# One shared group, one more SyncE group and later column starts in a message-passing layer whose rows come by four ways

## The chip, the cores and the metric

The kernel runs on one core of a Trainium2 chip. The metric is the device time of one execution in microseconds (us); three executions of the kernel before took 3390.92, 3395.1 and 3396.24 us, median 3395.1 us. The profile shows one more execution, which took 3398.46 us and whose span from the first to the last instruction is 3396.4 us. In the profile PE is TensorE, DVE is VectorE, ACT is ScalarE, POOL is GpSimd and SP is SyncE.

## The reference

A graph has N = 12,500 nodes with 128 features and E = 400,000 edges, sorted by their target `dst`, each with 32 features. One layer is computed:

```
h   = relu(layernorm(x))
m   = relu([h[src], h[dst], edge_attr] @ w1 + b1) @ w2 + b2      # one row for each edge
agg = segment_sum(m, dst)
gi, gh = agg @ w_ih + b_ih,  h @ w_hh + b_hh
r, z, n = sigmoid(i_r + h_r), sigmoid(i_z + h_z), tanh(i_n + r * h_n)
out = x + (1 - z) * n + z * h
```

## The kernel before

**Stages.** A first stage normalises the nodes, leaves h transposed on the chip (`hT_all`, 128 features by 12,500 nodes) and stores A = h @ w1[:128] and B = h @ w1[128:256] + b1 in device memory. Because `dst` is sorted, B's rows for an edge are taken from a short window of nodes. What remains per edge is a row of A at `src`, which is random access. The edges are cut in tiles of 128; eight tiles make a group k (`PAIR`), 391 groups in all (`NP`), the first with five tiles. The main loop has two units per group, `NU` = 782 units u, and a group k is worked on in units 2k and 2k+1, with its stages some units ahead.

**Four ways for the source rows.** The dictionary `mode` says for a group k who brings its rows:

- no entry: GpSimd gathers them with eight indirect DMAs (`gather`, L163), one per tile, into one of 11 buffers `G` (`GBUFS`). These groups are listed in `ring`; group i of the ring waits until group i - 11 has been used. The first nine groups (`RAW`) are gathered from x instead of A and normalised in the loop.
- `"act"`: ScalarE copies 1,024 columns of `hT_all`, one each instruction (L979, `one_by_one`), into a tile `HE_act`. The numbers of the columns come from the tile `at` by register loads, 16 at a time (L961).
- `"dve"`: VectorE does the same two columns at a time (L986, which packs two columns' bytes), loads 32 registers at a time, and after each 128 columns unpacks them into `HE_dve` (L991).
- `"sp"`: SyncE issues 1,024 DMAs of one 512-byte row of A each (L968), into the single buffer `G_sp`.

**What follows.** `pre` (L683, L694) forms the edge's pre-activation in PSUM: the window of B and the edge features by one matmul, and for `act` and `dve` groups also w1a against the columns brought. `add` (L713) is a VectorE operation that adds G and takes the relu for gathered and SyncE groups; for `act` and `dve` groups the relu is one ScalarE activation instead (L725, `relu`). `seg` (L739) sums by target with one-hot matrices made by VectorE (L586, L633); every 14 groups a block of nodes goes through the gates in small steps (`node`).

**Order.** Nothing is reordered: every engine takes its instructions as the program writes them. Which groups go to whom is fixed by `SPREAD` (how many groups each engine brings), `START` (the unit in which its first job begins) and the loop at L91, which spreads the groups of an engine evenly from `START`/2 + 2 to a last place. A job for group k runs from the end of the engine's job before it to unit 2k - 4 (SyncE: 2k - 8, and its next job begins at 2k + 2, since it has one buffer). `run_jobs` deals a job's steps out evenly over its units, in four phases a unit, between the other stages. The window rows (L613) and the tiles `L` (L574, L577) are also SyncE's, in the same queue as its rows.

Before, ScalarE brings 29 groups (16, 29, 42, 56, ... 374, 388), VectorE 28 (20, 34, 47, ... 372, 386), SyncE 4 (105, 197, 287, 379); 330 groups remain for GpSimd.

Of the kernel before, what the change touches and what calls it, by code (L numbers as in the profile page):

```python
# [9 lines left out]
F32 = mybir.dt.float32  # L10
# [14 lines left out]
PAIR = 2 * GRP  # L25
# [26 lines left out]
LOAD = {"act": 16, "dve": 32, "sp": 32}  # L52
PIECE = 128
STEP = {"act": 4, "dve": 8, "sp": 4}
ROW = 4 * D
SPREAD = {"dve": 28, "act": 29, "sp": 4}
START = {"dve": 10, "act": 2, "sp": 24}
NR = 12672

H_AT = 16512  # L60

# [2 lines left out]
def tile_gnn(ctx: ExitStack, tc: tile.TileContext, x, src, srcT, dstT, dstP, eaT, eaP, w1, b1, w2T, b2,  # L64
# [10 lines left out]
    pj = late.enter_context(tc.tile_pool(name="pj", bufs=2, side="right"))  # L75
# [12 lines left out]
        return [(t0 + a * GRP + j, j, a) for j in (2 * h, 2 * h + 1) for a in range(2)  # L88
                if t0 + a * GRP + j < t1]

    mode, order = {}, {m: [] for m in SPREAD}  # L91
    for m, n in SPREAD.items():
        lo, hi = START[m] // 2 + 2, NP - {"dve": 5, "act": 3, "sp": 12}[m]
        for i in range(n):
            k = lo + int((i + 1) * (hi - lo) / n)
            while k in mode:
                k += 1
            mode[k] = m
            order[m].append(k)


# [33 lines left out]
    stats = dram.tile([N, 2], F32, name="stats")  # L135
    S = dram.tile([NR, D + 1], F32, name="S")
    B = dram.tile([N, D], F32, name="B")
# [51 lines left out]
    nc.vector.memset(brow, 0.0)  # L189
    b1b = const.tile([128, D], F32, name="b1b")  # L190
    base_d = at[96:97, :NP - 1]
    by_hand = [k for m in ("sp", "act", "dve") for k in order[m]]
    NJ = len(by_hand)
    place_of = const.tile([NJ, 2], F32, name="place_of")
    for i, (to_sp, to_others) in enumerate(((ROW, 4), (0, H_AT))):
# [346 lines left out]
    def check_windows():  # L542
        m = const.tile([128, 2], F32, name="lim1")
        nc.vector.tensor_reduce(m[:, 0:1], lim[:, 0, :], AX.X, ALU.max)
        nc.vector.tensor_reduce(m[:, 1:2], lim[:, 1, :], AX.X, ALU.min)
        bad = const.tile([128, 2], F32, name="bad")
        nc.vector.tensor_scalar(bad[:, 0:1], m[:, 0:1], float(V - 1), None, op0=ALU.is_gt)
        nc.vector.tensor_scalar(bad[:, 1:2], m[:, 1:2], 0.0, None, op0=ALU.is_lt)
        one = const.tile([128, 1], F32, name="one")
        nc.vector.tensor_tensor(one, bad[:, 0:1], bad[:, 1:2], op=ALU.max)  # L550
        pm = SEGB[1][:, 384:512]
        nc.tensor.transpose(pm[0:1, :128], one, ident)
        f = const.tile([1, 8], F32, name="flags")
        nc.vector.tensor_reduce(f[:, 0:1], pm[0:1, :128], AX.X, ALU.max)
        nc.vector.tensor_reduce(f[:, 1:2], off_f, AX.XY, ALU.max)
        nc.vector.tensor_reduce(f[:, 2:3], step_f, AX.X, ALU.max)
        nc.vector.tensor_scalar(f[:, 3:4], blk_f[:, NB - 1:NB], float(N - BLOCKS[-1][2]), None,
                                op0=ALU.not_equal)
        nc.vector.tensor_copy(f[:, 4:5], beyond)
        nc.vector.tensor_reduce(f[:, 6:7], f[:, 0:5], AX.X, ALU.max)  # L560
        nc.vector.tensor_copy(flag, f[:, 6:7])
# [3 lines left out]
    hand = {}  # L565
# [380 lines left out]
    def column(v):  # L946
        return h_bytes[:, bass.ds(v - H_AT, 4)]

    def one_by_one(m, k):
        et = {"act": ET.Activation, "dve": ET.DVE, "sp": ET.SP}[m]  # L950
        r = by_hand.index(k)
        if m == "sp":
            goal[k] = tc.alloc_semaphore(f"brought{r}"), 16 * PAIR * 128
            G[k] = pj.tile([128, GRP, 2, D], F32, name="G_sp", bufs=1)
            rows = G[k].bitcast(U8)
        else:
            hand[k] = pj.tile([128, PAIR * 128], F32, name=f"HE_{m}")
            he = hand[k].bitcast(U8)
        for e0 in range(0, PAIR * 128, LOAD[m]):
            low, high = (0, ROW * (N - 1)) if m == "sp" else (H_AT, H_AT + 4 * (N - 1))  # L960
            _, vals = nc.values_load_multi_w_load_instructions(  # L961
                at[r:r + 1, e0:e0 + LOAD[m]], engines=[et], min_val=low, max_val=high,
                skip_runtime_bounds_check_because="src holds numbers of nodes")
            if m == "sp":
                for i, v in enumerate(vals):
                    e = e0 + i
                    a, j = divmod(e // 128, GRP)
                    fetched = nc.sync.dma_start(rows[e % 128:e % 128 + 1, j, a, :],  # L968
                                                A_bytes[bass.ds(v, ROW)].rearrange("(o f) -> o f", o=1))
                    fetched.then_inc(goal[k][0], 16)  # L970
                    tc.no_tile_sem_insts.add(fetched.ins.name)
                    tc.add_to_no_dep_group(f"rows{k}", fetched.ins)
                    if i % STEP[m] == STEP[m] - 1:
                        yield
                continue
            if m == "act":
                for i, v in enumerate(vals):
                    e = e0 + i
                    nc.scalar.copy(he[:, e * 4:e * 4 + 4], column(v))  # L979
                    if i % STEP[m] == STEP[m] - 1:  # L980
                        yield
                continue
            if e0 % PIECE == 0:
                both = pj.tile([128, PIECE // 2, 4], U16, name="both")
            for i in range(0, LOAD[m], 2):
                nc.vector.scalar_tensor_tensor(both[:, (e0 % PIECE + i) // 2, :], column(vals[i + 1]),  # L986
                                               256.0, column(vals[i]), op0=ALU.mult, op1=ALU.add)
                if i % STEP[m] == STEP[m] - 2:
                    if (e0 + i + 2) % PIECE == 0:
                        p0 = e0 + LOAD[m] - PIECE  # L990
                        nc.vector.tensor_copy(  # L991
                            he[:, p0 * 4:(p0 + PIECE) * 4].rearrange("p (n c b) -> p n c b", c=2, b=4),
                            both.bitcast(U8).rearrange("p n (b c) -> p n c b", c=2))
                    yield

    jobs = {}
    for m, kl in order.items():
        start = START[m]
        for k in kl:
# [3 lines left out]
    live = {}  # L1003
# [3 lines left out]
    def run_jobs(u, phase):  # L1007
        if phase == 0:
            for m, k, span in jobs.get(u, ()):
                live[m] = [one_by_one(m, k), u, span, PAIR * 128 // STEP[m], 0]  # L1010
        for m, job in list(live.items()):
            it, start, span, steps, done = job
            want = -(-steps * ((u - start) * PH + phase + 1) // (span * PH))
            while job[4] < want:
                job[4] += 1
                if next(it, "end") == "end":
                    del live[m]
                    break
# [56 lines left out]
    for u in range(NU):  # L1075
        k, h = divmod(u, 2)
        gathers(u)
        if h == 0:
# [14 lines left out]
            if k == NP - 20:  # L1093
                check_windows()
        if u == min(START.values()) - 2:
            nc.vector.tensor_scalar(at[:NJ, :], at[:NJ, :], place_of[:, 0:1], place_of[:, 1:2],
                                    op0=ALU.mult, op1=ALU.add)

        def other(phase):
            run_jobs(u, phase)  # L1100
            if h == 0 and phase == 3:
                take(k - 1)
            if phase == 3:
                step(nodes_left)
                if u in LAST_STEPS:
                    next(last)
# [114 lines left out]
    f = nc.values_load(flag[0:1, 0:1], min_val=0, max_val=1)  # L1221
# [67 lines left out]
```

## Time and profile before

| | us |
|---|---|
| median of three executions | 3395.1 |
| the profiled execution | 3398.46 |
| its span | 3396.4 |
| busy: PE / DVE / ACT / POOL | 2410.5 / 2254.8 / 3183.8 / 2536.6 |

A line of the profile's groups names the line of the code, the engine, the operation, its output and inputs, and how often it ran; then the time busy, the mean duration of one in ns, and the idle time of its engine just before it with what ended most of that. "Issue" is idle time that ended without anything that the profile shows; on VectorE and ScalarE the register loads of L961 lie in it, since they are not counted as busy. In a table of waits a row has the total, the number and the longest. A row of the timeline has the start, the duration, the instruction with its count, and the idle time before it in brackets. Busy time of copies that overlap in the pipeline is counted once, so the cost of one is the busy time divided by the count and not the mean duration.

### The profile page before, as it was taken

The page shows a single profiled execution, that of the slowest core. Times are in us where ns is not written, and L with a number is a line of the kernel's source. Part 1 is how long each engine was busy: PE and PEld are TensorE (multiplying, and loading weights), DVE is VectorE, ACT ScalarE, POOL GpSimd, SP SyncE. Part 2 cuts the span into 40 slices and gives each one's busy share as a digit, 9 for nine tenths or more (in the row PEclk, how much of TensorE's full clock was granted, in tenths as well). Part 3 has the DMA queues.
Part 4 walks back from the last instruction along what each step waited for, and adds up shares of the span by engine and source line. Part 5 has one row for each costly group of instructions (what it writes and reads, how often), then busy time and mean ns, then how long its engine had stood idle before and what let it go on. Part 6 is the DMA issues. An engine that isn't in the chain of part 4 may idle for free. (4 is left out here: it accounts for less than half of the span.)

```text
span 3396.4 us, 92978 instructions
## 1 busy us (share of the span) xinstructions
PE 2410.5 (71%) x13145; PEld 1547.7 (46%) x13145; DVE 2254.8 (66%) x16792; ACT 3183.8 (94%) x30083; POOL 2536.6 (75%) x2646
## 2 busy tenths in 40 slices
PE   7568767776677677677767776776676577767767
PEld 7445434444444344444444443454444344444445
DVE  8566667667666676676666666666666666666665
ACT  7699999999999999899999999999998999999995
POOL 7767777777777777777777777777777777777774
PEclk9777778877878788787778778777777887778878
DMA  6333444434434444343344343443443433444432
GB/s 214 97 85 87 101 99 95 99 94 106 95 96 98 99 97 96 95 103 95 92 100 97 92 100 94 102 93 97 97 102 87 101 94 94 100 100 96 94 94 62
DMA packets 194428, 334.67 MB, mean 99 GB/s; under 512 B 68293, under 2 KB 115972, under 8 KB 193809
## 3 DMA queue, kind: packets, MB, share of 16 engines
q0 software_dynamic: 84384, 172.99, 22.8%
q1 hardware_dynamic: 109281, 155.66, 17.2%
q14 instruction: 510, 4.18, 0.4%
q8 instruction: 109, 1.79, 0.2%
q10 hardware_dynamic: 144, 0.07, 0.0%
HBM read 308.21 MB, written 20.24 MB: 97 GB/s over the span
## 5 line engine op out<-in xcount | busy, mean ns | idle before, releaser
L163 POOL DMA_INDIRECT G<-A,src_i x2568 | 2469.5, 962 | 803.0 <-issue 761.5
L979 ACT COPY HE_act<-hT_all 128x4 uint8 x29696 | 2993.9, 189 | 52.9 <-issue 27.2
L986 DVE SCALAR_TENSOR_TENSOR both<-hT_all 128x4 uint16 x14336 | 1214.1, 154 | 990.4 <-issue 980.6
L683 PE MATMUL pre<-RW,L 128*128 128x256 f32 x3128 | 1130.2, 487 | 217.0 <-DVE RB L713 200.4
L683 PEld LDWEIGHTS pre<-RW,L 128*128 128x128 f32 x3128 | 662.5, 236 | 500.2 <-DVE RB L713 216.2
L739 PE MATMUL seg<-RB,OH 128*32 128x129 f32 x6250 | 609.4, 326 | 308.1 <-DVE RB L713 238.9
L739 PEld LDWEIGHTS seg<-RB,OH 128*32 128x32 f32 x6250 | 334.8, 126 | 802.2 <-DVE RB L713 460.3
L713 DVE CUSTOM_DVE_ANT_0 RB<-pre,G 128x1024 f32<-128x1024 f32 x322 | 389.4, 1210 | 26.0 <-PE pre L683 21.6
L734 PE MATMUL seg<-zrow 1*128 1x129 bf16 x196 | 45.9, 234 | 215.0 <-DVE OH L633 212.7
L586 DVE TENSOR_SCALAR L<-L,node_of 64x512 f32<-64x512 int32 x382 | 188.7, 494 | 10.7 <-DMA L<-in_dstP 10.7
L633 DVE TENSOR_TENSOR OH<-dloc,seg 128x512 f32<-128x512 f16 (+1 forms) x198 | 132.2, 668 | 0.0
L765 PE MATMUL nd<-spot,sums 128*128 128x40 f32 x782 | 114.5, 316 | 4.8 <-DVE sums L748 4.7
L765 PEld LDWEIGHTS nd<-spot,sums 128*128 128x128 f32 x782 | 109.8, 226 | 14.4 <-issue 8.8
L991 DVE COPY HE_dve<-both 128x512 uint8<-128x512 uint8 x224 | 102.4, 457 | 7.7
L848 PE MATMUL nd<-ident,gt 128*128 128x128 f32 (+2 forms) x112 | 28.5, 400 | 98.0 <-DVE gt L844 88.0
L694 PEld LDWEIGHTS pre<-w1a,HE_act 128*128 128x128 f32 x464 | 82.0, 221 | 9.5
L244 PE MATMUL nd<-w1b,hT_all 128*128 128x128 f32 x224 | 45.5, 346 | 56.5 <-DVE xb L850 56.5
L694 PEld LDWEIGHTS pre<-w1a,HE_dve 128*128 128x128 f32 x448 | 78.8, 220 | 9.2
L163 POOL DMA_INDIRECT G<-in_x,src_i x69 | 65.7, 952 | 21.9 <-issue 20.7
L694 PE MATMUL pre<-w1a,HE_act 128*128 128x128 f32 x464 | 80.5, 302 | 0.0
L725 ACT ACTIVATE RB<-pre 128x1024 f32<-128x1024 f32 x66 | 66.8, 1013 | 13.2 <-PE pre L694 13.2
L694 PE MATMUL pre<-w1a,HE_dve 128*128 128x128 f32 x448 | 77.7, 302 | 0.0
(177 smaller groups left out, 1374.9 us busy)
## 6 DMA issues: line engine op xcount, KB each, us to landing
G_sp<-A SPq DMA_DIRECT2D x4096, 0.5 KB
L<-in_dstP SPq DMA_DIRECT2D x195, 256.0 KB
L<-in_eaP SPq DMA_DIRECT2D x195, 256.0 KB
G<-A,src_i POOLq DMA_INDIRECT x2568, 2.6
RW<-B SPq DMA_DIRECT2D x782, 16.0 KB
xb<-in_x SPq DMA_DIRECT2D x26, 256.0 KB
out<-xb SPq DMA_DIRECT2D x26, 256.0 KB
xs<-in_x SPq DMA_DIRECT2D x11, 512.0 KB
```

Of the source, the lines that this page charges most:

```text
L163: fetched = nc.gpsimd.indirect_dma_start(out=G[k][:, j, a, :], out_offset=None, in_=table, in_offset=bass.IndirectOffsetOnAxis(ap=src_i[c] ...
L586: nc.vector.tensor_scalar(o, i, node_of[:, k:k + 1], None, op0=ALU.is_equal)
L633: nc.vector.tensor_tensor(p, dloc[:, e0:e1, None].to_broadcast(shape), row[:, None, :].to_broadcast(shape), op=ALU.is_equal)
L683: nc.tensor.matmul(p[:, 2 * i:2 * i + 2, :], Ls[k // QP][:, c0:c0 + 128], RW[k % 4], start=True, stop=not raw)
L694: nc.tensor.matmul(p[:, 2 * i + a, :], cols, w1a, start=False, stop=n + 1 == len(l) or l[n + 1][1] != j)
L713: made = nc.vector._custom_dve(TENSOR_ADD_SAT, out=o, in0=p, in1=G[k].rearrange("p j a f -> p (j a) f")[:, c, :], s0=float("inf"), s1=0.0)
L725: nc.scalar.activation(o, p, AF.Relu)
L739: nc.tensor.matmul(p[r0:r0 + V, :D + 1], OH[k][:, a * GRP + j, :], RB[k % 2][:, 2 * j + a, :D + 1], start=False, stop=all(b != a for _, _, ...
L765: nc.tensor.matmul(p[:, bass.ds(offs[i], V + SHIFT)], sums[:, slot(b, i), :D], spot[:, i % 2, :], start=False, stop=i == len(offs) - 1)
L979: nc.scalar.copy(he[:, e * 4:e * 4 + 4], column(v))
L986: nc.vector.scalar_tensor_tensor(both[:, (e0 % PIECE + i) // 2, :], column(vals[i + 1]), 256.0, column(vals[i]), op0=ALU.mult, op1=ALU.add)
L991: nc.vector.tensor_copy(he[:, p0 * 4:(p0 + PIECE) * 4].rearrange("p (n c b) -> p n c b", c=2, b=4), both.bitcast(U8).rearrange("p n (b c) ...
```

## The change

Group 197, before a SyncE group, becomes a shared one: ScalarE brings its first 512 columns and VectorE its last 512, into one tile `HE_dve`. ScalarE brings 28 whole groups beside it, VectorE 27, SyncE 5. The first job of VectorE begins in unit 14 instead of 10, that of ScalarE in unit 4 instead of 2. The places are now spread on either side of 197 separately. The number of groups that GpSimd gathers stays 330.

The places are now, for ScalarE: 17, 30, 43, 57, ... 177, 191, (197), 211, 225, ... 374, 388; for VectorE: 22, 36, 50, 64, ... 176, 190, (197), 210, 224, 237, ... 372, 386; for SyncE: 87, 160, 233, 307, 379. After 197 each group of VectorE stands one or two places before one of ScalarE.

```
-SPREAD = {"dve": 28, "act": 29, "sp": 4}
-START = {"dve": 10, "act": 2, "sp": 24}
+SPREAD = {"dve": 27, "act": 28, "sp": 5}
+START = {"dve": 14, "act": 4, "sp": 24}
+MIDDLE = 197
...
-    mode, order = {}, {m: [] for m in SPREAD}
+    mode, order = {MIDDLE: "both"}, {m: [] for m in SPREAD}
     for m, n in SPREAD.items():
         lo, hi = START[m] // 2 + 2, NP - {"dve": 5, "act": 3, "sp": 12}[m]
-        for i in range(n):
-            k = lo + int((i + 1) * (hi - lo) / n)
-            while k in mode:
+        n1, mid = (0, lo) if m == "sp" else (n // 2, MIDDLE)
+        places = [lo + int((i + 1) * (mid - lo) / (n1 + 0.5)) for i in range(n1)] + [MIDDLE] * (m != "sp")
+        for k in places + [mid + int((i + 1) * (hi - mid) / (n - n1)) for i in range(n - n1)]:
+            while k != MIDDLE and k in mode:
                 k += 1
-            mode[k] = m
+            mode.setdefault(k, m)
             order[m].append(k)
...
+    def share(m, k):
+        half = PAIR * 64
+        return (0, 2 * half) if k != MIDDLE else (0, half) if m == "act" else (half, 2 * half)
...
-            hand[k] = pj.tile([128, PAIR * 128], F32, name=f"HE_{m}")
+            if k not in hand:
+                hand[k] = pj.tile([128, PAIR * 128], F32, name="HE_dve" if k == MIDDLE else f"HE_{m}")
...
-        for e0 in range(0, PAIR * 128, LOAD[m]):
+        for e0 in range(*share(m, k), LOAD[m]):
...
-                live[m] = [one_by_one(m, k), u, span, PAIR * 128 // STEP[m], 0]
+                e0, e1 = share(m, k)
+                live[m] = [one_by_one(m, k), u, span, (e1 - e0) // STEP[m], 0]
```

More of the change, by code (lines that the diff above doesn't have):

```diff
@@ L191, in tile_gnn @@
     base_d = at[96:97, :NP - 1]
-    by_hand = [k for m in ("sp", "act", "dve") for k in order[m]]
+    by_hand = order["sp"] + order["act"] + [k for k in order["dve"] if k != MIDDLE]
     NJ = len(by_hand)
```

## The prediction

> **What bounds the kernel now.** I read the page's groups first, for what each engine does and how often.
>
> ```profile
> span 3396.4 us, 92978 instructions
> PE 2410.5 (71%) x13145; PEld 1547.7 (46%) x13145; DVE 2254.8 (66%) x16792; ACT 3183.8 (94%) x30083; POOL 2536.6 (75%) x2646
> L163 POOL DMA_INDIRECT G<-A,src_i x2568 | 2469.5, 962 | 803.0 <-issue 761.5
> L979 ACT COPY HE_act<-hT_all 128x4 uint8 x29696 | 2993.9, 189 | 52.9 <-issue 27.2
> L986 DVE SCALAR_TENSOR_TENSOR both<-hT_all 128x4 uint16 x14336 | 1214.1, 154 | 990.4 <-issue 980.6
> ```
>
> ACT looks like the limit at 94%. DVE has 980.6 us of "issue" besides its 2254.8 busy: that is its register loads, so it is near 95% too. POOL's 75% misleads: behind each gather stand some 0.3 us of issue. POOL's own timeline, with the line's own view, shows this:
>
> ```profile
> L163 POOL DMA_INDIRECT G<-A,src_i x2568: 942/947/1624, 92.9 to 3361.3; - x198
> DMA to landing us min/median/max: 2.5/2.7/5.5
> ...
> 215.62 0.95 POOL L163 DMA_INDIRECT G<-A,src_i  x1 [7.75 <-DVE RB L713]
> 216.87 0.95 POOL L163 DMA_INDIRECT G<-A,src_i  x1 [0.30 <-issue]
> ...
> 331.02 0.94 POOL L163 DMA_INDIRECT G<-A,src_i  x1 [4.36 <-DVE RB L713]
> ...
> 3361.32 0.95 POOL L163 DMA_INDIRECT G<-A,src_i  x1 [0.31 <-DMA G<-A,src_i]
> ```
>
> One gather starts every 1.25 us (216.87 - 215.62), and after 331.02 POOL never again stands still for a buffer: all its waits for anything but issue come before that. So POOL is a clock that runs through to 3361.32 whatever the others do. Who uses the rows?
>
> ```profile
> 3376.27 1.29 DVE L713 CUSTOM_DVE_ANT_0 RB<-pre,G 128x512 f32<-128x512 f32 x2 [3.12 <-PE pre L683]
> ...
> 3380.30 0.63 PE L739 MATMUL seg<-RB,OH 128*32 128x129 f32 x8
> ```
>
> The last group's rows land at about 3361.32 + 2.7 = 3364.0, and its add starts at 3376.27, released by PE and not by the landing. So the users of the rows are 12 us behind POOL at the end, and **they set the end**; POOL is just ahead. The windows and waits of the two long stretches, before and after group 197's place, say which user:
>
> ```profile
> 330.00:1710.00 1380.00, 993.19 (x5391) 622.77 (x5391) 928.54 (x7080) 1328.87 (x12929) 1047.52 (x1087) 0.79 0.41 97
> 1710.00:3330.00 1620.00, 1137.47 (x6226) 716.23 (x6226) 1076.97 (x8189) 1553.84 (x14986) 1229.31 (x1280) 0.79 0.40 97
> ...
> DVE both L986 <- issue: 424.1, 362, 2.4
> ACT gt L824 <- PE nd L818: 26.0, 7, 7.3
> PE seg L739 <- DVE RB L713: 119.9, 75, 5.0
> PE seg L739 <- ACT RB L725: 15.7, 6, 4.1
> ...
> DVE both L986 <- issue: 505.5, 415, 2.5
> PE seg L739 <- DVE RB L713: 113.0, 70, 7.6
> PE seg L739 <- ACT RB L725: 27.5, 10, 5.8
> ```
>
> The first four waits are of 330 to 1710, the last three of 1710 to 3330. DVE is taken for (928.54 + 424.1)/1380 = 98.0% of the first stretch and (1076.97 + 505.5)/1620 = 97.7% of the second, ACT for 96.3% and 95.9%. PE's `seg` waits for DVE some eight and four times as long as for ACT. So DVE limits, with ACT 2% behind it.
>
> **The change, part by part.** *Less work.* ScalarE's copy costs 2993.9/29696 = 0.101 us; 512 fewer are 51.6 us. Half a DVE group is 256 packing operations at 1214.1/14336 = 0.085 us, 16 register loads at 980.6/896 = 1.09 us (28 groups of 1,024 columns, 32 a load, are 896 loads) and four unpackings: 21.7 + 17.5 + 1.8 = 41 us.
>
> ```profile
> L991 DVE COPY HE_dve<-both 128x512 uint8<-128x512 uint8 x224 | 102.4, 457 | 7.7
> L713 DVE CUSTOM_DVE_ANT_0 RB<-pre,G 128x1024 f32<-128x1024 f32 x322 | 389.4, 1210 | 26.0 <-PE pre L683 21.6
> ```
>
> One group more is added by DVE (1.2 us), and ACT has one activation fewer. POOL keeps its 330 groups: nothing.
>
> *Where it goes.* The places decide. Before, DVE has a group every 13.5, ACT every 13.3. After, up to 197 DVE has one every 14 and ACT still one every 13.3; behind 197 DVE has one every 13.5 again and ACT one every 13.65. So **DVE is relieved in the first half alone and ACT in the second alone.** In the first stretch, 334 units (54 to 388), DVE gives up 1.1 of 37.8 columns a unit: 334 x 1.1 x 41/512 = 29 us. ACT is unchanged there and has 51 us idle (1380 - 1328.87), most of it such waits as the 26.0 at the gates, which a faster DVE shortens in part. The bounds are 0 and 51; I take 14, half of what DVE gives up, since ACT is 2% behind. In the second stretch, 376 units, ACT gives up 376 x 1.03 x 0.101 = 39 us and DVE takes up 4 (0.1 column a unit and the add). What ACT's relief can end is PE's 27.5 us of waits for it, and DVE stands between: from 4 us worse to 24 us better, taken as 9.
>
> *The later starts.* ACT is full early on:
>
> ```profile
> 137.00:215.00 78.00, 52.91 (x332) 42.39 (x330) 47.61 (x310) 77.73 (x609) 52.80 (x55) 0.81 0.32 81
> 215.00:330.00 115.00, 85.73 (x441) 52.76 (x439) 73.81 (x563) 114.03 (x1107) 83.88 (x88) 0.77 0.37 86
> ```
>
> Two units without copies take 2 x 39 x 0.101 = 7.9 us from it before the wait that ended at 215.62; without copies such a unit is left to the normalising chain, so I take half, 4, with 0 and 7.9 as bounds. DVE's four units gain nothing while ACT is full. POOL gains too: the wait that ended at 215.62 shrinks by 4, and the one at 331.02 goes, since one hand-brought group instead of two now stands before the buffer in question, and an earlier add frees it: 4.36 - 0.30 = 4.1. POOL ends 8 us earlier (bounds 4 and 12).
>
> *SyncE.* Its queue carries the window rows and L too, so what it adds counts:
>
> ```profile
> 1608.55 3.55 SPq L968 DMA_DIRECT2D G_sp<-A  x10
> ...
> L961 SPq TENSOR_LOAD <-at x128: 1872/2148/2357, 238.4 to 3247.9; - x128
> ...
> SPq L574 <- PE pre L683: 407.1, 94, 14.9
> SPq L613 <- PE pre L683: 165.4, 36, 19.1
> SPq L574 <- PE pre L694: 71.5, 16, 12.3
> ```
>
> A row costs 3.55/10 = 0.355 and a 32nd of a 2.15 us load: 0.42 us, a group 432 us. SyncE's waits for PE, time in which it is early, are 407.1 + 165.4 + 71.5 = 644 us. They hide it, with 212 us left over; where a stretch lacks cover, L and the window rows come late, and `onehot_T` on DVE and `pre` on PE wait for them. L is asked for six units ahead, 6 x 4.13 us (1380/334), so I take nothing; the price if the cover is gone is a rival below.
>
> *Group 197.* ACT brings 512 columns in 12 units, 42.7 a unit instead of some 37.5: 6 us late at most, once, and one unit of slack stands behind it. PE waits for two engines where it waited for one. Nothing to 6 us; I take nothing.
>
> *The sum.* The users of the rows: 4 + 14 + 9 = 27 us, which would end the span at 3369. But POOL now stands in front of them. Its last gather starts at 3361.32 - 8 = 3353.3, lands at 3356.0, is added by 3357.3 (1.29), and from the first `seg` of the last group to the end stand 3396.4 - 3380.30 = 16.1 us: **3373.4 is the floor.** The two routes are nearly equal, and users that run close to POOL's landings lose some to each wait; half of a group's time, 5 us, is my allowance. 3378.5 is 18 us under the span. The profiled execution took 3398.46, 3.4 over the median of 3395.1, so I take the 18 us from the median: about 3378.
>
> The Trainium skill, "DMA: Bandwidth & Descriptors", section "Issuing engines are not separate DMA queues", says that DMAs from SyncE and GpSimd run on the same 16 engines and interleave, which speaks against 1,024 more rows. By that rule the last landing could be up to 5.5 instead of 2.7 us behind its gather, and the floor 3 us later; the windows' DMA share of 0.41 and 0.40, with four SyncE groups already under way, gives it little weight.
>
> **The rivals.**
>
> *No difference.* The engine that is not relieved holds each half: ACT the first (it is at 96.3%), DVE the second (97.7%). For it: each has under 4% idle. Against: PE waits little for ACT in the first half. Then only the early 4 us and a few are won: 3391, between 3388 and 3400.
>
> *Slower: SyncE becomes the limit.* Its jobs of 1,024 rows last 170 to 178 units before and 134 to 142 after, so it issues up to 7.5 rows a unit instead of 6.
>
> ```profile
> 1607.33 1.12 SPq L613 DMA_DIRECT2D RW<-B  x2
> ```
>
> At 0.42 us a row 7.5 rows are 3.15 us; the window rows are 1.12 us for two units, and I take as much again for L and the nodes' DMAs less a tenth, 1 us a unit: 4.15 us of the first half's 4.13. That little is carried by the lead of some 20 us with which L and the window rows are asked for, and each job begins anew. It decides from about 0.44 us a row, where 136 units run late by more than the lead. At 0.46 the first two jobs lose 6 and 23 us (142 x 0.18 - 20, 136 x 0.32 - 20), and PE and DVE wait as long: 3395 + 29 = 3424, from 3402 up. The second half's units, 1620/376 = 4.31 us, still have room. Against: the 644 us of early time.
>
> *ACT alone is the limit.* Then all of its 51.6 us come back: 3343. Against: POOL's clock, which would have to end 30 us earlier than it can. The Trainium skill, "Perfetto Trace Analysis", section "Identifying the Most-Contended Engine", names the engine with the highest occupancy, here ACT at 94%, as the one to relieve; the trace disagrees by POOL's unbroken spacing of 1.25 us at 75%.
>
> *The change does not do what it says*: half a group late at 197 costs more than it saves. Once 6 us against 27: it ends as no difference.
>
> **How the numbers follow.** The forecast, POOL and the users near each other: 0.62, from 3368 (POOL's waits all but gone, 12 us, and no allowance) to 3387. No difference, with 197's delay: 0.22, of which 0.04 falls just under 3388 and 0.02 over 3402. SyncE: 0.11. ACT alone: 0.02. Left over: 0.03, to either side. 0.2% is 6.8 us, about what a measurement of this kernel can tell from no change. Faster is 0.62 + 0.04 + 0.02 + 0.02 = 0.70, the same 0.16, slower 0.11 + 0.02 + 0.01 = 0.14. The range reaches from 3368 to 3398, over most of the rival of no difference.
>
> **What the next profile would show.** If right: POOL's last gather starts near 3353, its wait near 215 is about 4 us shorter and the one near 331 gone; the last group's add follows its landing within a few us; DVE's taken share falls in the first half, ACT's in the second; SyncE's waits for PE fall from 644 to about 200 us; VectorE has begun to wait for landings. Wrong, if DVE or PE wait for L or RW by more than 20 us in all, if PE's waits at group 197's matmuls exceed 6 us, or if the lag at the last add stays at 12 us.

## The result, and the profile after

The changed kernel takes 3382.5 us (median of 6 runs, 3379.91 to 3388.39), beside 3395.67 us for the kernel before on the same chip (6 runs, 3390.92 to 3402.74). The ratio is 0.9961, with a 95% interval of 0.9946 to 0.9976: **13.2 us or 0.39% faster**. The forecast was 3378, in a range of 3368 to 3398. The profiled execution took 3383.67 us; it was 3398.46 before.

The page of the changed kernel, first its busy times, then its groups (lines were added to the file: L163 is now L165, L613 is L615, L713 is L715, L739 is L741, SyncE's row L968 is L975, ScalarE's copy L979 is L986 and VectorE's L986 is L993):

```profile
span 3381.8 us, 94224 instructions
PE 2384.9 (71%) x13129; PEld 1538.3 (45%) x13129; DVE 2230.9 (66%) x16533; ACT 3132.6 (93%) x29570; POOL 2532.8 (75%) x2646
L165 POOL DMA_INDIRECT G<-A,src_i x2568 | 2465.5, 960 | 787.1 <-issue 762.3
L986 ACT COPY HE_act<-hT_all 128x4 uint8 x28672 | 2889.2, 189 | 50.6 <-issue 26.8
L993 DVE SCALAR_TENSOR_TENSOR both<-hT_all 128x4 uint16 x14080 | 1192.8, 154 | 969.4 <-issue 961.2
```

The removed work is there at the foretold size: VectorE has 21.3 us fewer of packing and 19.4 fewer of register loads, ScalarE 51 fewer in all (512 of its copies now write `HE_dve` and aren't in the line above). POOL's idle time fell from 803.0 to 787.1 us, and its gathers together from 2469.5 to 2465.5. That makes POOL 19.9 us earlier. Most of it is its waits for buffers, before and after:

```profile
POOL G L163 <- DVE RB L713: 16.4, 14, 7.7
...
POOL G L165 <- DVE RB L715: 2.8, 7, 1.0
```

The two waits of 7.75 and 4.36 us that the prediction named are both gone. The timeline, POOL's last gather and VectorE's last add, shows where this leads:

```profile
3341.53 0.94 POOL L165 DMA_INDIRECT G<-A,src_i  x1 [0.30 <-issue]
...
3360.73 1.29 DVE L715 CUSTOM_DVE_ANT_0 RB<-pre,G 128x512 f32<-128x512 f32 x2 [3.10 <-PE pre L685]
```

The last gather starts 19.8 us earlier than before (3361.32), the last add only 15.5 (3376.27). With 2.7 us to landing, the median of the kernel before, the add comes 16.5 us behind its rows, where it was 12.3. So the users of the rows still set the end, and POOL is farther ahead of them than it was.

The windows of the two long stretches (span, then busy us of PE, PEld, DVE, ACT, POOL, granted clock, DMA share, GB/s), and the waits in them, first those of 330 to 1710, then those of 1710 to 3330:

```profile
330.00:1710.00 1380.00, 965.19 (x5449) 613.55 (x5446) 922.20 (x6947) 1340.11 (x13025) 1047.70 (x1090) 0.81 0.42 99
1710.00:3330.00 1620.00, 1148.61 (x6194) 721.82 (x6194) 1068.83 (x8143) 1503.72 (x14503) 1229.38 (x1282) 0.78 0.41 97
```

```profile
DVE both L993 <- issue: 399.0, 344, 2.9
DVE L L588 <- DMA L<-in_dstP: 42.1, 16, 6.4
...
PE pre L685 <- DMA RW<-B: 145.6, 42, 7.3
...
PE seg L741 <- DVE RB L715: 57.6, 37, 4.2
...
PE seg L741 <- ACT RB L727: 35.5, 12, 6.1
...
DVE both L993 <- issue: 517.0, 410, 2.6
...
ACT gt L826 <- PE nd L820: 67.6, 14, 11.8
```

In the first stretch VectorE's taken share fell from 98.0% to (922.20 + 399.0)/1380 = 95.7%, as foretold, but a new wait for the tiles L, 42.1 us, brings it to 98.8%. PE waits less for VectorE (57.6 us, before 119.9), and 145.6 us for window rows (RW in the lines). Both L and the window rows are SyncE's. In the second stretch VectorE is as full as before, (1068.83 + 517.0)/1620 = 97.9%, while ScalarE has gone from 95.9 to 92.8%: its relief turned up as waiting, 67.6 us of it at the gates (28.6 before). PE waits there for window rows too, 34.7 us, where before it had no such wait.

SyncE's own waits for PE in the first stretch say why L came late. Before:

```profile
SPq L574 <- PE pre L683: 151.9, 37, 14.9
SPq L613 <- PE pre L683: 36.9, 12, 9.1
...
SPq L574 <- PE pre L694: 22.2, 6, 7.6
```

After:

```profile
SPq L576 <- PE pre L685: 11.3, 8, 5.1
SPq L615 <- PE pre L685: 5.1, 1, 5.1
```

Of 211.0 us in which SyncE was early 16.4 are left, 194.6 fewer. The rows that it issued in this stretch, before and after:

```profile
L968 SPq DMA_DIRECT2D G_sp<-A x1894: 224/228/706, 330.0 to 1709.8; - x190
...
L975 SPq DMA_DIRECT2D G_sp<-A x2356: 212/228/561, 329.8 to 1709.3; - x197
```

The 462 rows more, at the prediction's 0.42 us a row, are 194 us, just what SyncE lost of its early time. The prediction set its new load against the 644 us of the whole kernel. Over the whole kernel its sum holds well (109.7 + 88.6 + 36.3 = 235 us are left of 644, some 200 were foretold), and in the first stretch it fails.

A table of where the users stand, from the starts of a group's add in each trace, after less before in us (negative is earlier). SP4, STARTS, DVE27 and ACT28 are experiments below:

```
group      9     60    100    140    168    208    300    340    390
after  -11.6  -11.0  -20.7  -10.9  -12.8  -19.9  -22.2  -19.8  -15.5
SP4     -8.5  -17.7  -31.1  -31.7  -34.4  -31.7  -37.3  -28.3  -16.1
STARTS -11.4   -1.9   -4.2    8.1    8.8    7.3   -3.5   -3.1    3.0
DVE27  -12.8  -10.3  -21.1  -16.0  -19.6  -31.8  -44.9  -41.3  -23.5
ACT28  -11.6   -4.5     --    7.3     --   14.9   -0.5    0.9    4.1
```

(In ACT28 the groups 100 and 168 are ScalarE's and have no such add.) Each row is one execution, and where the places of the groups differ it swings by some 10 us from group to group, so it is good for the large differences alone. The profiled execution of ACT28 took 3403.79 us, 10 under that kernel's median; the others lie within 3.5 us of theirs.

The changed kernel has 11.6 us by the first add, has 9 more by group 100, has lost these by group 140, and then wanders about its value.

### The profile page after: what moved, and what is told of

It is laid out like the page before. It is cut to its first block, busy times and chain, and to the rows that moved or that the text cites. A ratio compares the mean times of both kernels' runs of the same rounds, so it can differ in the third digit from the quotient of the medians.

```text
span 3381.8 us, 94224 instructions
## 1 busy us (share of the span) xinstructions
PE 2384.9 (71%) x13129; PEld 1538.3 (45%) x13129; DVE 2230.9 (66%) x16533; ACT 3132.6 (93%) x29570; POOL 2532.8 (75%) x2646
## 5 line engine op out<-in xcount | busy, mean ns | idle before, releaser
L165 POOL DMA_INDIRECT G<-A,src_i x2568 | 2465.5, 960 | 787.1 <-issue 762.3
L986 ACT COPY HE_act<-hT_all 128x4 uint8 x28672 | 2889.2, 189 | 50.6 <-issue 26.8
L993 DVE SCALAR_TENSOR_TENSOR both<-hT_all 128x4 uint16 x14080 | 1192.8, 154 | 969.4 <-issue 961.2
L741 PE MATMUL seg<-RB,OH 128*32 128x129 f32 x6250 | 597.1, 321 | 278.7 <-DVE RB L715 215.4
L741 PEld LDWEIGHTS seg<-RB,OH 128*32 128x32 f32 x6250 | 329.5, 124 | 668.2 <-DVE RB L715 342.2
L715 DVE CUSTOM_DVE_ANT_0 RB<-pre,G 128x1024 f32<-128x1024 f32 x322 | 389.6, 1210 | 23.4 <-PE pre L685 23.2
L588 DVE TENSOR_SCALAR L<-L,node_of 64x512 f32<-64x512 int32 x382 | 186.8, 489 | 53.2 <-DMA L<-in_dstP 53.2
L696 PEld LDWEIGHTS pre<-w1a,HE_dve 128*128 128x128 f32 x448 | 84.8, 235 | 10.7
L826 ACT ACTIVATE gt<-nd 128x512 f32<-128x512 f32 (+2 forms) x28 | 16.4, 586 | 77.9 <-PE nd L820 77.8
L165 POOL DMA_INDIRECT G<-in_x,src_i x69 | 65.9, 955 | 21.9 <-issue 20.7
```

Source lines behind the costliest of these rows:

```text
L165: fetched = nc.gpsimd.indirect_dma_start(out=G[k][:, j, a, :], out_offset=None, in_=table, in_offset=bass.IndirectOffsetOnAxis(ap=src_i[c] ...
L588: nc.vector.tensor_scalar(o, i, node_of[:, k:k + 1], None, op0=ALU.is_equal)
L696: nc.tensor.matmul(p[:, 2 * i + a, :], cols, w1a, start=False, stop=n + 1 == len(l) or l[n + 1][1] != j)
L715: made = nc.vector._custom_dve(TENSOR_ADD_SAT, out=o, in0=p, in1=G[k].rearrange("p j a f -> p (j a) f")[:, c, :], s0=float("inf"), s1=0.0)
L741: nc.tensor.matmul(p[r0:r0 + V, :D + 1], OH[k][:, a * GRP + j, :], RB[k % 2][:, 2 * j + a, :D + 1], start=False, stop=all(b != a for _, _, ...
```

## The experiments

The theory after the result: VectorE is the limit, what is taken from it counts, and SyncE's fifth group takes part of it back by bringing L late. The rivals: the starts alone make the gain; ScalarE's relief makes it; the fifth SyncE group costs nothing. Each comparison is with the kernel before on the same chip.

**Starts only** (STARTS). The kernel before with the later starts alone:

```
-START = {"dve": 10, "act": 2, "sp": 24}
+START = {"dve": 14, "act": 4, "sp": 24}
```

> The kernel before with the later starts alone (VectorE 14, ScalarE 4); 29, 28 and 4 groups as before. In the changed kernel the first add stands 11 us earlier and the last 15. Theory 'SyncE late' (the later starts give about 11 us, the relief of VectorE and ScalarE would give more, but the fifth SyncE group makes L and the window rows late and takes it back): 3395.7 - 11 = about 3385. Rival 'starts alone' (the group moved to SyncE gives nothing at all): the whole gain, 3382 to 3383. The recorded sum had 4 us for this part: 3392.

Measured: 3402.97 us beside 3397.76, ratio 1.0012 [1.0000, 1.0023]: no gain. The end in its timeline:

```profile
3350.65 0.95 POOL L163 DMA_INDIRECT G<-A,src_i  x1 [0.30 <-issue]
...
3379.23 1.29 DVE L713 CUSTOM_DVE_ANT_0 RB<-pre,G 128x512 f32<-128x512 f32 x2 [3.11 <-PE pre L683]
```

POOL ends 10.7 us earlier than before and the users 3 us later. The first add is 11.4 us earlier, but of that 1.9 are left at group 60. So an earlier POOL by itself is worth nothing, and none of the figures expected came out: the starts don't make the gain alone.

**Old starts in the changed kernel.** The changed kernel with START as before (10 and 2).

> The changed kernel with the old starts (VectorE 10, ScalarE 2); the shared group 197 and five SyncE groups stay. Theory 'SyncE late': only what the moved group nets, some 3 us: 3392. Rival 'starts alone': no gain, 3396. By the recorded sum, in which the moved group was worth 23 us against POOL's floor, 3382 to 3386.

Measured: 3392.49 us, ratio 0.9985 [0.9972, 0.9999]. That is the figure of the theory. VectorE's waits for L are much as in the changed kernel (53.2 in all there):

```profile
DVE L L588 <- DMA L<-in_dstP: 42.7, 11, 10.8
```

With the starts the ratio is 0.9961, without 0.9985: within the change they are worth some 8 to 10 us (two chips, and intervals that touch each other, so the size is rough). The same edit that gave nothing alone pays where VectorE has fewer columns.

**VectorE relieved, ScalarE not** (DVE27). The kernel before with the new starts, no shared group, and a whole group taken from VectorE:

```
-SPREAD = {"dve": 28, "act": 29, "sp": 4}
-START = {"dve": 10, "act": 2, "sp": 24}
+SPREAD = {"dve": 27, "act": 29, "sp": 5}
+START = {"dve": 14, "act": 4, "sp": 24}
```

> The kernel before with the later starts and one whole group moved from VectorE to SyncE (27, 29, 5), all spread evenly, no shared group. VectorE is lighter by 82 us over the whole length, ScalarE as before. Theory 'SyncE late': below e1 by only a few us, and VectorE's waits for L and PE's for RW as long as in the changed kernel (42 and 180 us) or longer. Rival 'VectorE limits and the moved group pays': below e1 by 10 us or more, at POOL's floor of 3372 to 3375.

**ScalarE relieved, VectorE not** (ACT28). The same with the group taken from ScalarE:

```
+SPREAD = {"dve": 28, "act": 28, "sp": 5}
```

> The same with the whole group moved from ScalarE (28, 28, 5). ScalarE is lighter by 103 us, VectorE as in e1. Theory 'SyncE late': the same as e1 or slower, since VectorE, which limits, gains nothing and L comes late. Rival 'ScalarE limits': below e1 by 10 us or more.

Measured: from VectorE 3377.68 us, 0.9938 [0.9922, 0.9955]; from ScalarE 3414.09, 1.0044 [1.0027, 1.0061]. Both have five SyncE groups and 330 of POOL. The first, the waits of VectorE and then its end in the timeline:

```profile
DVE RB L713 <- DMA G<-A,src_i: 49.9, 25, 5.7
DVE L L586 <- DMA L<-in_dstP: 39.3, 15, 10.7
```

```profile
3347.79 0.95 POOL L163 DMA_INDIRECT G<-A,src_i  x1 [0.30 <-DMA G<-A,src_i]
...
3352.74 1.29 DVE L713 CUSTOM_DVE_ANT_0 RB<-pre,G 128x512 f32<-128x512 f32 x2 [3.13 <-PE pre L683]
```

VectorE now waits for landings, 25 times, and the last add is 3352.74 - 3347.79 - 2.7 = 2.3 us behind the last one. This kernel has reached POOL's floor; the changed kernel has not. Of the expectations the rival's is nearer, 25 us below the starts alone, though a little over its range. The waits for L are there as the theory said, 39.3 us (and 162.3 of PE for window rows), and cost less than VectorE's lighter load brings. The second, its first stretch in the windows and the waits in that and in the whole:

```profile
330.00:1710.00 1380.00, 991.35 (x5327) 623.17 (x5323) 921.82 (x7012) 1272.68 (x12358) 1047.42 (x1091) 0.80 0.41 98
```

```profile
DVE both L986 <- issue: 426.4, 355, 2.4
...
PE seg L739 <- DVE RB L713: 310.0, 164, 7.5
```

ScalarE is idle for 107 us of 1380 and VectorE is taken for (921.82 + 426.4)/1380 = 97.7%. A whole group less for ScalarE, and the kernel is slower; PE's `seg` waits 310.0 us for VectorE, where it waited 238.9 in the kernel before. **Of the two VectorE limits.** By its groups, with the new starts and five SyncE groups: 28 give 3414.09, 27.5 give 3382.5, 27 give 3377.68 (the middle one on another chip and with other places). ScalarE had 28, 28.5 and 29. The two runs of this pair have the same SyncE and POOL groups and starts, and lie 36 us apart. What ScalarE's relief is worth without a fifth SyncE group wasn't tried. Nor is it shown why ACT28 is 11 us slower than the starts alone: VectorE waits only 11.9 us for L in it, and PE 72.8 for window rows.

**Four runs on a chip with another limit.** The next four fell on a chip on which the kernel before took 5790.88 us (18 runs) and so say little of this question. Four SyncE groups in the changed kernel (`"sp": 4`):

> The changed kernel with four SyncE groups instead of five; group 197 stays shared, VectorE 27.5, ScalarE 28.5 groups, and GpSimd gathers 331 groups instead of 330. GpSimd's clock gets 8 x 1.266 = 10 us longer: its last gather near 3351.6, the floor by the run of one group less for VectorE (last gather 2.7 + 2.3 us before the last add, 20.4 us from there to the end) near 3377 of span. Theory 'SyncE late costs time' (in the changed kernel VectorE waits 53 us for L and PE 190 us for window rows): the waits fall to the 11 and 17 us of before, the users of the rows gain in the first half, and the time is at the floor, 3378 to 3380, in spite of the extra gathers. Theory 'VectorE's own work limits and the waits for L stand in for others': the users keep their pace, 3382 to 3385.

VectorE relieved with the old starts (SPREAD 27, 29, 5, START as before):

> One whole group from VectorE to SyncE as in the run before, but with the old starts (10 and 2). Theory 'the later starts are worth what GpSimd no longer waits': where VectorE has room, GpSimd's clock is the end, and the old starts bring its early waits back, 8 to 15 us: 3386 to 3392. Rival 'the starts are worth nothing' (as with the starts alone): 3376 to 3380.

The kernel before with ScalarE's later start alone (`"act": 4`):

> The kernel before with ScalarE's later start alone (4), VectorE's stays 10. Theory 'work put off is packed closer' (with both starts later the first add came 11 us earlier and all of it was lost by group 60, since VectorE, which limits, had the same columns to bring in fewer units): the early gain stays, since VectorE's columns keep their density: 3385 to 3389. Rival: what comes early is always lost later, 3395 to 3403.

The changed kernel with ScalarE's 29th whole group beside the shared one (`"act": 29`; 329 groups of POOL):

> The changed kernel with one whole ScalarE group more (29.5, VectorE 27.5, SyncE 5), so that GpSimd gathers 329 groups. GpSimd's clock gets 10 us shorter, ScalarE 103 us heavier (3 per cent of its time). Theory 'VectorE limits, ScalarE has room': no slower than the changed kernel, 3378 to 3383. Rival 'ScalarE is as near its limit': 3400 or more.

Measured there: 5769.62 us, 0.9956 [0.9940, 0.9973]; 5880.07, 1.0142 [1.0119, 1.0166]; 5769.91, 0.9957 [0.9940, 0.9974]; 5830.15, 1.0063 [1.0041, 1.0085]. What differs there shows in the waits of the first of them:

```profile
ACT HE_act L986 <- issue: 2109.7, 2995, 2.1
...
POOL G L165 <- DVE RB L715: 2162.7, 218, 43.7
```

ScalarE stands still between its copies for 2109.7 us with nothing to wait for (26.8 in the changed kernel), and POOL, far ahead, waits 2162.7 us for buffers. With ScalarE standing still like this, the order of the kernels is another. The first three were run again at the usual pace; the fourth wasn't and stays open.

**Four SyncE groups in the changed kernel, again** (SP4). One edit; POOL has 331 groups then:

```
-SPREAD = {"dve": 27, "act": 28, "sp": 5}
+SPREAD = {"dve": 27, "act": 28, "sp": 4}
```

> The kernel of e5 again, on a chip that runs at the usual pace, one hopes. Four SyncE groups, GpSimd 331, VectorE 27.5, ScalarE 28.5. Theory 'SyncE late costs time': VectorE's waits for L fall from 53 to some 11 us and PE's for window rows from 190 to some 17, and the time goes to GpSimd's floor, now 10 us later: 3378 to 3380. Theory 'VectorE's own work limits, the waits for L stand in for others': 3382 to 3386.

Measured: 3385.95 us beside 3396.1, ratio 0.9966 [0.9953, 0.9979], as the changed kernel within the intervals. Its waits of VectorE and PE, and the end in the timeline:

```profile
DVE RB L715 <- DMA G<-A,src_i: 20.4, 10, 4.5
DVE L L588 <- DMA L<-in_dstP: 11.0, 2, 10.8
...
PE pre L685 <- DMA RW<-B: 22.9, 3, 12.4
```

```profile
3356.52 0.94 POOL L165 DMA_INDIRECT G<-A,src_i  x1 [0.30 <-issue]
...
3360.20 1.29 DVE L715 CUSTOM_DVE_ANT_0 RB<-pre,G 128x512 f32<-128x512 f32 x2 [3.11 <-PE pre L685]
```

The waits for L and the window rows are gone, 53 to 11 and 190 to 23 us over the whole kernel, and by the table the users stand at -34 us at group 168 where the changed kernel stands at -13: **by group 168 SyncE's lateness costs 22 us.** That is read at group 168 because behind it POOL holds SP4 back: group 174's last gather starts at 1534.20 and its add at 1539.79, 2.9 us behind the landing, and by group 208 the two kernels are 12 us apart. At the end POOL's last gather starts 15 us later than in the changed kernel, 10 of them the eight gathers more, and the last add sits 1.0 us behind its landing. The fifth SyncE group gives POOL time and takes it from the users; at the end the two are worth the same. The waits came out as the theory said, but its time, 3378 to 3380, was missed: it had POOL's last gather near 3351.6, which started at 3356.52. The measured time falls in the range of the rival, whose mechanism (the users keep their pace) the table speaks against.

**VectorE relieved, old starts, again.** The kernel before with one line changed, SPREAD 27, 29, 5:

> The kernel of e7 again: one whole group from VectorE to SyncE with the old starts. Theory 'where VectorE has room, GpSimd's clock is the end and the later starts are worth its early waits': 8 to 15 us above e3, 3386 to 3392, last gather near 3356. Rival 'the starts are worth nothing': 3376 to 3380.

Measured: 3375.17 us, ratio 0.9935 [0.9921, 0.9949]. This is the **fastest version**, though not told from DVE27 by its interval; that lies under the changed kernel's but for 0.0003, on another chip. VectorE waits as long for L and PE for window rows as in the changed kernel, 45.0 and 202.9 us: the whole group taken from VectorE outweighs them. POOL's last gather and the last add, in an execution that took 3368.35 us, 7 under the median:

```profile
3348.83 0.95 POOL L163 DMA_INDIRECT G<-A,src_i  x1 [0.30 <-DMA G<-A,src_i]
...
3351.41 0.69 DVE L713 CUSTOM_DVE_ANT_0 RB<-pre,G 128x512 f32<-128x512 f32 x1 [4.19 <-DMA G<-A,src_i]
```

The add waits 4.19 us for the landing itself. By the times the starts are worth nothing here (0.9938 with, 0.9935 without), so the theory's 3386 to 3392 was missed, and neither a shared group nor later starts are needed for the gain. The traces are less plain: as the theory said, the old starts bring POOL's idle time back (798.9 us, 788.7 in DVE27), but the 2568 gathers together took 8.8 us less (2461.2 and 2470.0), so that the last one starts only 1 us later. Why they took less isn't shown.

**ScalarE's later start alone, again.** The kernel before with `"act": 4`:

> The kernel of e8 again: the kernel before with ScalarE's later start alone. Theory 'work put off is packed closer' (VectorE limits, and with its own start later the same columns came in fewer units): with VectorE's start unchanged the early gain stays, 3385 to 3389. Rival 'what comes early is always lost later': 3395 to 3403.

Measured: 3391.67 us beside 3396.1, ratio 0.9982 [0.9972, 0.9992], between the two ranges. In the profile the first add is 6.3 us earlier, the last 8.5. So the gain of ScalarE's two units lasts, 4.4 us; it is VectorE's four units that spoil the starts in the kernel before. That VectorE's columns, which must then stand closer, are the reason was argued from its 98%, and not tried by itself.

**Six SyncE groups** in the changed kernel (`"sp": 6`):

> The changed kernel with six SyncE groups instead of five (GpSimd 329, VectorE 27.5, ScalarE 28.5): a job of 1,024 rows has 108 to 116 units, 9.1 rows a unit instead of 7.5. Theory 'SyncE late costs time': SyncE needs 9.1 x 0.39 + 1.04 + 0.14 = 4.7 us a unit where the users take 4.2, over 676 units 340 us, less what the lead of some 20 us in each job carries: 3600 to 3720, VectorE's waits for L and PE's for window rows several hundred us. Theory 'the waits for L stand in for others': about 3380, GpSimd's clock 10 us shorter.

Measured: 3720.78 us beside 3396.4, ratio 1.0962 [1.0933, 1.0991]. Its waits of VectorE and PE:

```profile
DVE L L588 <- DMA L<-in_dstP: 344.6, 106, 10.3
...
PE pre L685 <- DMA RW<-B: 798.8, 166, 11.1
```

The theory's 3600 to 3720 is met at its upper end. The rival of the prediction, SyncE as the limit, is real, and stands one group away.

## Why the prediction was right or wrong

**The bound** (users of the rows set the end, VectorE first, ScalarE a little behind): right. A group moved from VectorE to SyncE makes the kernel 0.62% faster, one from ScalarE 0.44% slower. The rule that was cited against it, "Identifying the Most-Contended Engine" in the Trainium skill's "Perfetto Trace Analysis", to relieve the engine of highest occupancy, doesn't hold here: ScalarE was that engine, at 94%, and the kernel that relieves it is 36 us slower than the one that relieves VectorE, at 66%. VectorE's register loads, which the busy time leaves out, bring it to 98% in the first stretch of the kernel before.

**The removed work:** right to 2 us.

**VectorE's half, 14 us:** too small by itself. Without SyncE's lateness (SP4) the users win 26 us from group 9 to 168, where 29 were given up over groups 27 to 194. In the changed kernel they win 1 us over the same groups: SyncE takes nearly all of it back.

**ScalarE's half, 9 us:** failed. Its relief became waiting (the second stretch of the profile after, and ACT28), and VectorE is as full there as before. From group 208 to 390 the changed kernel loses 4 us; how much of that is SyncE's, with PE's 34.7 us of waits for window rows, isn't separated. The offsets swing by 10 us on the way, and why it doesn't hold the -20 to -22 that it has at 208 and 300 stays open.

**The starts, 4 us:** mis-sized. The first add came 11.6 us earlier, and within the change they are worth 8 to 10 us. ScalarE's two units alone are worth 4.4, much as forecast. VectorE's four, put at nothing, take that away in the kernel before, where both starts together give nothing; that was missed.

**SyncE, nothing:** this is the step that failed most. "SyncE's waits for PE ... 644 us ... They hide it" held the cover of the whole kernel against a load that falls unevenly: in the first stretch there were 211 us, and 195 of them went. The kernel met two signs that were named for being wrong: over 20 us of waits for L or window rows (53 and 190), and a lag at the last add that didn't shrink from 12 us (16.5). The sum of the SyncE rival, 4.15 us of 4.13 a unit, had the place right; it let the lead carry what had cost the users 22 us by group 168.

**Group 197, nothing:** right, as far as can be seen. In PE's timeline of the changed kernel its first matmuls:

```profile
1735.70 1.19 PE L685 MATMUL pre<-RW,L 128*128 128x256 f32 x2 [5.40 <-DMA RW<-B]
1736.68 1.06 PE L696 MATMUL pre<-w1a,HE_dve 128*128 128x128 f32 x4
```

PE waits for window rows, SyncE's again. That alone doesn't clear the halves, since ScalarE's last copy for the group starts at 1734.5, only 1.2 us before. In SP4, where the group is shared in the same places and the window rows come in time, PE goes on without a wait:

```profile
1719.86 1.22 PE L685 MATMUL pre<-RW,L 128*128 128x256 f32 x2
1720.88 1.06 PE L696 MATMUL pre<-w1a,HE_dve 128*128 128x128 f32 x4
```

**"POOL now stands in front":** wrong for this kernel. POOL's last gather started at 3341.5 and not at 3353, outside the bounds of 4 to 12 us earlier, as the wait near 215 went whole and not by 4 us, and the gathers took 4.0 us less together. The users won 15.5 us and not 27. The floor by the prediction's own sum is 3341.53 + 2.7 + 1.29 + 16.1 = 3361.6, 20 us under the span. The floor itself exists: DVE27, SP4 and the fastest version stand on it within some 2 us, while VectorE has no wait for a landing in the changed kernel. The later landing that was weighed after the Trainium skill's "DMA: Bandwidth & Descriptors", section "Issuing engines are not separate DMA queues", can't be read at the end: SyncE issues its last row of A at 3259.8 us in the changed kernel and at 3246.7 in the fastest version, long before the last gather. In the latter the add that waits for the last landing starts 3351.41 - 3348.83 = 2.6 us after the gather. No run here shows what the rows do to a landing while they are under way. So the time came out 5 us from the forecast because the users fell short by about what the floor and the allowance had cut off; that nearness is partly luck.

**The rivals:** no difference (3391, a ratio of 0.9986) lies outside the interval, but its mechanism came true in the second half, where VectorE, at 97.9%, turned ScalarE's relief into waiting. ScalarE alone (3343) falls with ACT28. That half a group late at 197 eats the gain falls with PE's waits in SP4. SyncE's mechanism came at a lower price than 29 us, and behind a gain large enough to hide it.

## What to carry to other kernels

Set the cover of an in-order queue against its new load stretch by stretch; a sum over the kernel hides the stretch in which it runs out, and behind that edge the price is steep (one group more than in the changed kernel: 338 us). Which of two engines near 95% limits is found by taking work from each in turn, and register loads count as work although they aren't counted as busy. When a producer runs as a clock, earlier rows are worth nothing until its users can follow, and faster users nothing once they stand on it: look at the lag of the last use behind its landing first.

## What the hardware did that was not expected

One chip ran the same kernels at 5770 to 5880 us. ScalarE's single copies there often start 0.7 or 1.4 us apart, with nothing to wait for, as in this part of the timeline of the changed kernel with four SyncE groups:

```profile
1002.51 0.19 ACT L986 COPY HE_act<-hT_all 128x4 uint8 x1 [1.20 <-issue]
1003.91 0.19 ACT L986 COPY HE_act<-hT_all 128x4 uint8 x1 [1.21 <-issue]
1004.63 0.19 ACT L986 COPY HE_act<-hT_all 128x4 uint8 x1 [0.52 <-issue]
```

At the usual pace a copy costs 0.101 us. The mean granted TensorE clock was 0.667 there, beside 0.80 in the changed kernel's profile. The cause isn't shown.
